# Fixing the order of the attention's matmuls on TensorE in a fused conv, attention and norm kernel

## Chip, cores, metric

The kernel runs on one core of one Trainium2 chip. The metric is the device time of one execution in microseconds (us), the median of several runs. All data are float32.

## What is computed

Eight images `x[8, 512, 32, 32]` go through two layers, each with a residual. Layer 0 normalises the image in groups, splits it by a 1x1 convolution (`cv1`) into two halves of 256 channels, runs two blocks on the second half, each a 3x3 convolution, an attention over the 1024 pixels with 4 heads of 64 channels, and a 1x1 convolution, and joins the four halves by a 1x1 convolution (`cv2`). Layer 1 normalises and applies one 1x1 convolution with a masked and permuted weight. Cut to what matters here:

```python
def bot_attention(x, qkv_w, rw, rh):
    q, k, v = (qkv[:, 0], qkv[:, 1], qkv[:, 2])
    logits = jnp.einsum('bhdi,bhdj->bhij', q, k + r) * HD ** (-0.5)
    a = jax.nn.softmax(logits, axis=-1)
    out = jnp.einsum('bhij,bhdj->bhdi', a, v)
...
    ys = [t[:, :C], t[:, C:]]
    for i in range(N):
        z = cbs(ys[-1], m_cv1_w[i], m_cv1_bn[i], 1)
        z = bot_attention(z, m_qkv_w[i], m_rw[i], m_rh[i])
        z = jax.nn.silu(bn_eval(conv2d(z, m_cv2_w[i], 0), m_cv2_bn[i]))
        ys.append(ys[-1] + z)
    return cbs(jnp.concatenate(ys, axis=1), cv2_w, cv2_bn, 0)
...
x = x + L0(groupnorm(x))
x = x + L1(groupnorm(x))
```

## The kernel before

**Units.** The attention is cut into 64 units (class `Unit`): image, block, pair of heads and half of the queries (512 of 1024). Sixteen slots of four units each follow one another; a slot is one block of one image. A unit works on eight tiles of 128 keys (`KT = 8`). Each step works on two heads at once, as two matmuls on two halves of the array: `logits` (L502) contracts 64 rows, and its two heads lie in the upper and the lower 64 rows; `values` (L548) and `finish` (L560) write 64 columns, and their two heads lie in the left and the right 64 columns. In the profile a float32 matmul shows as two instructions, so that `logits(t)` and `values(t)` are four instructions each and `finish` is four; `top` and `spread` are eight transposes each.

**What a unit does.** `logits(t)` makes two banks `lg`; ScalarE copies them to `st` (L508) and VectorE takes the running maximum `mx` (L513). `top` transposes the maximum on TensorE (`mt`, L521) and VectorE reduces it (`nm`, L522); `spread` transposes it back as a row for every key (`mb`, L529). `soften` adds it (VectorE, L533), `exponent` takes the exponential on ScalarE (L537) and adds up the sum on GpSimd (L542), `values` accumulates the output `po` over the eight tiles (L548). `finish` adds the sum over the keys on TensorE (`den`, L560), ScalarE copies it (L562), and `divide` takes the reciprocal (L566) and multiplies on VectorE.

**The emitted order.** The loop at the end of the kernel writes the work of unit `u`, of the unit `before` it and of the one after it (`nxt`) in this order: `u.top()`, filler, `u.spread()`, filler, and then, for t = 0, 2, 4, 6: at t = 0 `before.finish()`; `u.soften(t)`, `u.soften(t + 1)`; `values(t - 2)`, `values(t - 1)` (at t = 0 the last two tiles of `before`); at t = 0 `before.divide`; `nxt.logits(t)`, `nxt.logits(t + 1)`; the exponents; filler. So on TensorE, without the filler, a unit is emitted as mt, mb, den, and then four times values and logits.

**The filler.** Everything else on TensorE (the convolutions, `project`, `conv_m2`, `cv1`, `cv2` and the last layer) is cut into pieces by generators, and `advance(share)` emits as many pieces as the share of the slot's planned time asks for. The pieces between two steps of the attention are thus planned by the costs that the generators yield, and a plan's overrun can leave a place without a piece.

**Who sets the final order.** The emitted order is not the executed one. A scheduler goes through the program with its own estimate of durations, and where the next instruction in emitted order isn't ready it takes a later one of the same engine that is. Two chains of order edges (`add_manual_dep` with `IN_ORDER`, a dependency without a semaphore) already fix what may not be moved: `in_turn` for VectorE (L513, L533 and the transforms of `Spread`) and `act_turn` for ScalarE (L508, L537). TensorE has no such chain.

**Accumulators.** Of the eight banks, `ps_m` has two (`mb`), `ps_o` one (`po`) and `ps_f` five. The five of `ps_f` serve `lg` (four for a pair of tiles), `mt`, `den` and all the filler; a bank comes free when its last reader is done.

Of the kernel before, what the change touches and what calls it, by code (L numbers as in the profile page):

```python
# [20 lines left out]
IN_ORDER = mybir.DependencyInfo(mybir.DependencyClass.NoSync, mybir.DependencyReason.DATA)  # L21

P = 128
# [5 lines left out]
HALF = 512  # L29
NBLK = 2  # L30
HD = 64
NG = 16
KT = 8
# [6 lines left out]
def conv_preact_kernel(ctx: ExitStack, tc: tile.TileContext, x, cv1, cv2, mcv1, qkv, mcv2, bn, rw, rh, conv, s_in, t_in, out):  # L40
    nc = tc.nc
# [23 lines left out]
    def pair(p, tag, name):  # L65
        return p.tile([P, 2, HALF], F32, tag=tag, name=name)

    def bank(name):
        return ps_f.tile([P, HALF], F32, tag="bank", name=name)

    def half_tile(name):
        return tp.tile([P, HALF], F32, tag="t", name=name)
# [27 lines left out]
    ident = const.tile([P, P], F32, name="ident")  # L100
    make_identity(nc, ident)
    ones = const.tile([P, P], F32, name="ones")
# [79 lines left out]
    def in_turn(instruction):  # L182

        if turn:
            tc.add_manual_dep(instruction.ins, turn.pop().ins.name, IN_ORDER, reason="order of VectorE")
        turn.append(instruction)

    def act_turn(instruction):

        if act_last:  # L190
            tc.add_manual_dep(instruction.ins, act_last.pop().ins.name, IN_ORDER, reason="order of ScalarE")
        act_last.append(instruction)

    act_last = []

    class Spread:

# [288 lines left out]
    class Unit:  # L486
# [8 lines left out]
        def logits(self, t):  # L495

            if t == 0:
                self.begin()
            lg = [bank(f"lg_{self.name}_{t}_{h}") for h in range(2)]
            for h in range(2):  # L500
                r = slice(HD * h, HD * h + HD)
                nc.tensor.matmul(  # L502
                    lg[h], self.k[r, ts(t, P)], self.q[r, self.hp, ts(self.half, HALF)], start=True, stop=True
                )
            st = pair(stp, "st", f"st_{self.name}_{t}")
            self.st.append(st)
            for h in range(2):
                act_turn(nc.scalar.copy(st[:, h], lg[h]))  # L508
            if t == 1:
                self.mx = pair(one, "mx", f"mx_{self.name}")  # L510
            for h in range(2 if t else 0):
                so_far = self.st[0] if t == 1 else self.mx
                in_turn(nc.vector.tensor_tensor(self.mx[:, h], so_far[:, h], lg[h], ALU.max))  # L513

        def top(self):

            self.nm = small.tile([P, 2, 4], F32, tag="nm", name=f"nm_{self.name}")
            for h in range(2):
                mt = bank(f"mt_{self.name}_{h}").rearrange("p (c i) -> p c i", i=P)
                for c in range(4):  # L520
                    nc.tensor.transpose(mt[:, c], self.mx[:, h, ts(c, P)], ident)  # L521
                nc.vector.tensor_reduce(self.nm[:, h], mt, AX.X, ALU.max, negate=True)  # L522

        def spread(self):

            self.mb = pair(ps_m, "mb", f"mb_{self.name}")
            for h in range(2):
                for c in range(4):
                    nc.tensor.transpose(self.mb[:, h, ts(c, P)], self.nm[:, h, c : c + 1].to_broadcast([P, P]), ident)  # L529

        def soften(self, t):
            st = flat(self.st[t])
# [11 lines left out]
        def values(self, t):  # L544
            if t == 0:
                self.po = ps_o.tile([P, HALF], F32, tag="po", name=f"po_{self.name}")
            for h in range(2):
                nc.tensor.matmul(  # L548
                    self.po[HD * h : HD * h + HD],
                    self.v[:, t, ts(h, HD)],  # L550
                    self.st[t][:, h],
                    start=(t == 0),
                    stop=(t == KT - 1),
                )

        def finish(self):

            den = bank(f"den_{self.name}")
            for h in range(2):
                nc.tensor.matmul(den[HD * h : HD * h + HD], ones[:, :HD], self.acc[:, h], start=True, stop=True)  # L560
            self.rb = half_tile(f"rb_{self.name}")
            nc.scalar.copy(self.rb, den)  # L562

# [56 lines left out]
    def tables():  # L620
# [8 lines left out]
        sc = s_sb.rearrange("p a k g -> p (a k) g")  # L629
        cols = small.tile([P, 4, 2 * CT], F32, tag="cols", bufs=1, name="cols")  # L630
        top, rsum, gain, idx = (cols[:, j] for j in range(4))

        def wide(v):
            return v.unsqueeze(2).to_broadcast(full)

        e, oh, lower = scr[:, 1], scr[:, 2], scr[:, 3]
        nc.vector.tensor_reduce(top, sc, AX.X, ALU.max)
        nc.vector.tensor_tensor(e, sc, wide(top), ALU.subtract)
        nc.scalar.activation(e, e, AF.Exp)
        nc.vector.tensor_reduce(rsum, e, AX.X, ALU.add)  # L640
# [489 lines left out]
```

## Times and profile before

| what | us |
|---|---|
| three runs | 3197.96, 3199.95, 3203.04 |
| median | 3199.95 |
| the profiled execution, whole | 3202.86 |
| its span, first to last instruction | 3201.1 |
| TensorE busy | 3115.6 (97%) |
| VectorE busy | 2076.9 (65%) |
| ScalarE busy | 1718.5 (54%) |
| GpSimd busy | 1244.7 (39%) |

The granted clock of TensorE was 0.993 over the span. The groups of instructions that the change touches, of the profiled execution (two instructions a float32 matmul, and the two heads at the same time, so that the busy time is that of the pair):

| line, what | count | busy us | mean ns |
|---|---|---|---|
| L502 `lg` | 2048 | 522.4 | 617 |
| L548 `po` | 2048 | 516.6 | 607 |
| L560 `den` | 256 | 85.0 | 618 |
| L529 `mb` | 512 | 67.7 | 275 |
| L521 `mt` | 512 | 66.6 | 273 |

In a timeline of the profile a row is a run of like instructions on one engine: its start from the beginning of the span, how long it took, the engine and line, the operation, what it writes and reads, the shape, the number of instructions, and in brackets the idle time before it with what ended it. Rows of one engine may overlap a little at their ends[...]; the time that a run occupies is read from its start to the next start.

### The profile page before, as it was taken

What the parts mean: (1) busy time and instruction counts of PE and PEld (TensorE: products, weight loads), DVE (VectorE), ACT (ScalarE), POOL (GpSimd) and SP (SyncE); (2) the same over time, 40 slices, a digit from 0 to 9 for tenths busy, and PEclk for the clock granted to TensorE, in tenths of its full rate; (3) what the DMA queues carried; (4) which work ended last, traced back from release to release, by engine and by line L of the source; (5) the groups of instructions that cost most, each with busy time, mean ns of one, the idle gap of its engine ahead of it and who ended that gap; (6) DMA issues with size and microseconds to landing.
All of it is one profiled execution on the core that took longest, in us unless ns stands there. A gap on an engine that the chain in (4) does not pass through costs nothing.

```text
span 3201.1 us, 33271 instructions
## 1 busy us (share of the span) xinstructions
PE 3115.6 (97%) x11668; PEld 1527.5 (48%) x11668; DVE 2076.9 (65%) x2718; ACT 1718.5 (54%) x2347; POOL 1244.7 (39%) x971
## 2 busy tenths in 40 slices
PE   7999999999999999999999999999999999999999
PEld 3645444454445454454445454454445454453343
DVE  5446576668666676667666686667766676666642
ACT  3255765854645555544656455554645555556631
POOL 2114334445434354344434444345434443344420
PEclk9999999999999999999999999999999999999999
DMA  8851442421233232424233332424233241413366
GB/s 293 290 182 63 154 159 83 148 78 64 89 109 129 92 118 70 139 85 138 89 112 132 109 122 70 145 83 136 95 112 125 98 139 55 159 63 122 106 220 217
DMA packets 142007, 399.29 MB, mean 125 GB/s; under 512 B 13072, under 2 KB 14352, under 8 KB 141840
## 3 DMA queue, kind: packets, MB, share of 16 engines
q1 hardware_dynamic: 141120, 396.94, 36.3%
q8 instruction: 92, 1.51, 0.2%
q14 instruction: 75, 0.61, 0.1%
q10 hardware_dynamic: 720, 0.23, 0.0%
HBM read 317.42 MB, written 79.69 MB: 124 GB/s over the span
## 4 chain that ended last, share of the span: by engine, by line
PE 71%; DVE 7%; ACT 4%; DMA 2%; issue 2%; POOL 0%; SPq 0%; ACTq 0%; DVEq 0%
PE m L305 14%; PE cv L175 13%; PE po L548 11%; PE lg L502 11%; PE l L175 6%; PE qk L175 6%; PE v L397 3%; PE den L560 2%; PE m L175 2%; DVE st L533 2%; PE mb L529 2%; PE mt L521 2%; ACT st L508 1%; DVE mx L513 1%; ACT st L537 1%
## 5 line engine op out<-in xcount | busy, mean ns | idle before, releaser
L542 POOL TENSOR_TENSOR sum<-sum,st 128x512 f32<-128x512 f32 x768 | 996.8, 1323 | 705.6 <-ACT st L537 705.4
L513 DVE TENSOR_TENSOR mx<-mx,lg 128x512 f32<-128x512 f32 x768 | 477.2, 681 | 412.2 <-ACT st L508 412.2
L537 ACT ACTIVATE st<-st 128x1024 f32<-128x1024 f32 x512 | 539.1, 1068 | 341.7 <-DVE st L533 340.4
L508 ACT COPY st<-lg 128x512 f32<-128x512 f32 x1024 | 524.6, 596 | 350.5 <-PE lg L502 336.4
L533 DVE TENSOR_TENSOR st<-st,mb 128x1024 f32<-128x1024 f32 x512 | 603.2, 1212 | 66.5 <-PE mb L529 66.5
L305 PE MATMUL m<-plane,w_m 128*128 128x256 f32 x2304 | 534.4, 386 | 15.7 <-ACT cv2s L130 8.9
L548 PE MATMUL po<-st,v 128*64 128x512 f32 x2048 | 516.6, 607 | 18.3 <-ACT st L537 18.2
L502 PE MATMUL lg<-q,k 64*128 64x512 f32 x2048 | 522.4, 617 | 2.3 <-ACT y L130 1.7
L305 PEld LDWEIGHTS m<-plane,w_m 128*128 128x128 f32 x2304 | 431.3, 191 | 144.7 <-issue 47.0
L542 POOL TENSOR_TENSOR sum<-st,st 128x512 f32<-128x512 f32 x128 | 165.2, 1312 | 822.7 <-ACT st L537 822.7
L175 PE MATMUL cv<-y,w_cv 128*128 128x512 f32 x1024 | 463.2, 598 | 6.2 <-DVE mx L513 4.5
L502 PEld LDWEIGHTS lg<-q,k 64*128 64x128 f32 x2048 | 180.8, 186 | 333.5 <-issue 264.3
L175 PEld LDWEIGHTS cv<-y,w_cv 128*128 128x128 f32 x1024 | 186.3, 190 | 248.7 <-issue 230.6
L548 PEld LDWEIGHTS po<-st,v 128*64 128x64 f32 x2048 | 131.9, 137 | 328.4 <-issue 238.1
L175 PE MATMUL l<-x,w_l 128*128 128x512 f32 x512 | 235.9, 604 | 9.1 <-DVE mx L513 9.1
L175 PE MATMUL cv<-x,w_cv 128*128 128x512 f32 x512 | 235.1, 607 | 8.3 <-ACT x L165 2.4
L175 PE MATMUL qk<-z,w_qkv 128*128 128x512 f32 x512 | 234.0, 600 | 1.5 <-DVE mx L513 1.5
L566 DVE RECIPROCAL rb<-rb 128x256 f32<-128x256 f32 x128 | 215.4, 1722 | 29.5 <-ACT rb L562 29.4
L522 DVE TENSOR_REDUCE nm<-mt 128x4 f32<-128x512 f32 x128 | 82.4, 684 | 157.7 <-PE mt L521 157.7
L562 ACT COPY rb<-den 128x512 f32<-128x512 f32 x64 | 37.3, 584 | 233.4 <-PE den L560 233.4
L175 PEld LDWEIGHTS l<-x,w_l 128*128 128x128 f32 x512 | 92.8, 190 | 133.5 <-issue 110.8
L175 PEld LDWEIGHTS cv<-x,w_cv 128*128 128x128 f32 x512 | 95.0, 193 | 128.1 <-issue 107.9
(145 smaller groups left out, 2451.8 us busy)
## 6 DMA issues: line engine op xcount, KB each, us to landing
w_m<-w_m SPq DMA_DIRECT2D x96, 768.0 KB, 4.7
w_cv<-in_cv SPq DMA_DIRECT2D x90, 512.0 KB, 3.5
y<-y SPq DMA_DIRECT2D x64, 512.0 KB, 5.0
x<-in_x SPq DMA_DIRECT2D x56, 512.0 KB, 5.4
y<-y SPq DMA_DIRECT2D x64, 256.0 KB, 3.4
k<-r SPq DMA_DIRECT2D x32, 512.0 KB, 3.6
res<-y SPq DMA_DIRECT2D x32, 512.0 KB, 4.0
xr<-in_x SPq DMA_DIRECT2D x32, 512.0 KB, 4.1
```

The costliest lines, as they stand in the source:

```text
L175: nc.tensor.matmul(ps, w, moving, start=(n == 0), stop=(n == len(terms) - 1))
L305: nc.tensor.matmul(ps[:, ts(co, 256)].rearrange("p (t x) -> p t x", x=F), w[:, co, c, dx], u[:, 9 * c : 9 * c + 8, dx : dx + F], start=(j ...
L397: nc.tensor.matmul(ps[:, ts(j, P)], z[:, c, ts(4 * j4 + j, P)], w[:, c, 512 + P * hp : 512 + P * hp + P], start=(c == 0), stop=(c == IT - 1),)
L502: nc.tensor.matmul(lg[h], self.k[r, ts(t, P)], self.q[r, self.hp, ts(self.half, HALF)], start=True, stop=True)
L508: act_turn(nc.scalar.copy(st[:, h], lg[h]))
L513: in_turn(nc.vector.tensor_tensor(self.mx[:, h], so_far[:, h], lg[h], ALU.max))
L522: nc.vector.tensor_reduce(self.nm[:, h], mt, AX.X, ALU.max, negate=True)
L533: in_turn(nc.vector.tensor_tensor(st, st, flat(self.mb), ALU.add))
L537: act_turn(nc.scalar.activation(st, st, AF.Exp))
L542: nc.gpsimd.tensor_tensor(self.acc[:, h], so_far[:, h], self.st[t][:, h], ALU.add)
L548: nc.tensor.matmul(self.po[HD * h : HD * h + HD], self.v[:, t, ts(h, HD)], self.st[t][:, h], start=(t == 0), stop=(t == KT - 1),)
L566: nc.vector.reciprocal(self.rb[:, r], self.rb[:, r])
```

## The change

A third chain of order edges, `pe_turn`, is made for TensorE, and every matmul and transpose of the class `Unit` is passed through it. Each of them gets an edge to the one emitted just before it. No instruction, operand, tile or semaphore wait of the program text is added or taken away, and the filler is not in the chain. The diff, without the lines that are only indented anew:

```diff
     act_last = []
+
+    def pe_turn(instruction):
+
+        if pe_last:
+            tc.add_manual_dep(instruction.ins, pe_last.pop().ins.name, IN_ORDER, reason="order of TensorE")
+        pe_last.append(instruction)
+
+    pe_last = []
...
-                nc.tensor.matmul(
-                    lg[h], self.k[r, ts(t, P)], self.q[r, self.hp, ts(self.half, HALF)], start=True, stop=True
+                pe_turn(
+                    nc.tensor.matmul(
+                        lg[h], self.k[r, ts(t, P)], self.q[r, self.hp, ts(self.half, HALF)], start=True, stop=True
+                    )
                 )
...
-                    nc.tensor.transpose(mt[:, c], self.mx[:, h, ts(c, P)], ident)
+                    pe_turn(nc.tensor.transpose(mt[:, c], self.mx[:, h, ts(c, P)], ident))
...
-                    nc.tensor.transpose(self.mb[:, h, ts(c, P)], self.nm[:, h, c : c + 1].to_broadcast([P, P]), ident)
+                    pe_turn(
+                        nc.tensor.transpose(self.mb[:, h, ts(c, P)], self.nm[:, h, c : c + 1].to_broadcast([P, P]), ident)
+                    )
...
-                nc.tensor.matmul(
-                    self.po[HD * h : HD * h + HD],
+                pe_turn(
+                    nc.tensor.matmul(
+                        self.po[HD * h : HD * h + HD],
...
-                nc.tensor.matmul(den[HD * h : HD * h + HD], ones[:, :HD], self.acc[:, h], start=True, stop=True)
+                pe_turn(
+                    nc.tensor.matmul(den[HD * h : HD * h + HD], ones[:, :HD], self.acc[:, h], start=True, stop=True)
+                )
```

More of the change, by code (lines that the diff above doesn't have):

```diff
@@ L547, in values @@
             for h in range(2):
-                nc.tensor.matmul(
-                    self.po[HD * h : HD * h + HD],
[L550 to L553, printed above, removed]
+                pe_turn(
+                    nc.tensor.matmul(
+                        self.po[HD * h : HD * h + HD],
+                        self.v[:, t, ts(h, HD)],
+                        self.st[t][:, h],
+                        start=(t == 0),
+                        stop=(t == KT - 1),
+                    )
                 )
@@ L559, in finish @@
             for h in range(2):
-                nc.tensor.matmul(den[HD * h : HD * h + HD], ones[:, :HD], self.acc[:, h], start=True, stop=True)
+                pe_turn(
+                    nc.tensor.matmul(den[HD * h : HD * h + HD], ones[:, :HD], self.acc[:, h], start=True, stop=True)
+                )
             self.rb = half_tile(f"rb_{self.name}")
```

## The prediction

> **What bounds the kernel now.** I read the page first, then TensorE's waits, then its timeline unit by unit.
>
> ```profile
> span 3201.1 us, 33271 instructions
> ...
> PE 3115.6 (97%) x11668; PEld 1527.5 (48%) x11668; DVE 2076.9 (65%) x2718; ACT 1718.5 (54%) x2347; POOL 1244.7 (39%) x971
> ```
>
> ```profile
> PE po L548 <- ACT st L537: 18.2, 16, 2.9
> ...
> PE l L175 <- DVE mx L513: 9.1, 7, 2.1
> ```
>
> TensorE is busy for 97%, and it works through the tail too, so time that it gains in one place is not lost later as long as it is fed. Its own waits are short: the largest sum is 18.2 us, values waiting for an exponential. The other line (seven waits, 9.1 us in all, the longest 2.1) is filler of the last layer waiting for the reader of a bank that logits held; convolutions wait for it in the same way. So what counts is how well the busy time is used. A unit in emitted order (its part around mb, from TensorE's timeline at 1562 us):
>
> ```profile
> 1565.08 1.04 PE L529 MATMUL mb<-ident,nm 128*128 128x128 f32 x8
> 1565.95 1.88 PE L175 MATMUL cv<-y,w_cv 128*128 128x512 f32 x4
> 1567.76 1.08 PE L560 MATMUL den<-sum,ones 128*64 128x512 f32 x4
> 1568.67 1.89 PE L548 MATMUL po<-st,v 128*64 128x512 f32 x8
> 1570.49 1.99 PE L502 MATMUL lg<-q,k 64*128 64x512 f32 x8
> ```
>
> And one in another order (timeline from 1249 us):
>
> ```profile
> 1249.88 1.04 PE L521 MATMUL mt<-ident,mx 128*128 128x128 f32 x8
> 1250.84 1.07 PE L560 MATMUL den<-sum,ones 128*64 128x512 f32 x2
> 1251.85 1.09 PE L529 MATMUL mb<-ident,nm 128*128 128x128 f32 x8
> 1252.86 0.64 PE L560 MATMUL den<-sum,ones 128*64 128x512 f32 x1
> ...
> 1255.58 3.46 PE L502 MATMUL lg<-q,k 64*128 64x512 f32 x12
> 1259.86 2.02 PE L548 MATMUL po<-st,v 128*64 128x512 f32 x8 [0.81 <-ACT st L537]
> 1261.81 1.13 PE L502 MATMUL lg<-q,k 64*128 64x512 f32 x4
> 1262.87 5.42 PE L175 MATMUL cv<-y,w_cv 128*128 128x512 f32 x12
> ```
>
> See the counts: `den` comes as 2, 1, 1 instead of 4, and 12 and 4 `lg` stand where 8 and 8 were emitted. One head's `den` fills the wait for `nm` between mt and mb, and logits fill the wait for the exponential. In 40 of 64 units the order is the emitted one; 24 deviate.
>
> [...] a pair of heads starts 7 ns apart, and the next pair 429 ns later, the same 429 ns that one full matmul instruction takes; so a head without its partner costs its 0.86 us (two instructions) for half the work. [...] `po` to `lg` has 522 ns from start to start, 93 more than 429. [...]
>
> ```profile
> 1337.75 1.97 PE L548 MATMUL po<-st,v 128*64 128x512 f32 x2 [2.85 <-ACT st L537]
> 1339.65 6.19 PE L305 MATMUL m<-plane,w_m 128*128 128x256 f32 x18
> ```
>
> 18 instructions take 6.19 us, where 24 of them take 5.45 us elsewhere (1502.81 us); the granted clock from 1337.7 to 1344.0 is 0.51.
>
> **The change part by part.** It adds no instruction and no semaphore; it moves matmuls of `Unit` back to emitted order. They issue no DMA. Filler that takes their place is moved forward, with its readers on ScalarE and VectorE, and the weight loads behind it on SP; SP's queue isn't what TensorE waits for (all its DMA waits I found are under 0.6 us), so I cost that at nothing. What is new is that the wait of `values` or of mb now also holds the logits and `den` queued behind it, and with late logits the copies (0.6 us each) and maxima (0.68 us) of the next unit. It costs time only where no filler is at hand.
>
> (a) The split `den`. From den to lg 4.74 us (1250.84 to 1255.58), mb included; in order 0.87 (mb) + 2.73 (1567.76 to 1570.49) = 3.60. With 0.09 more at mt (0.96 against 0.87), 1.23 us a unit. Fourteen units have it, at 543, 722, 884, 1250, 1440, 1480, 1610, 1975, 2163, 2203, 2334, 2700, 2888 and 2926 us; 756 has a variant.
>
> (b) Logits ahead of values. Whole tiles (12 and 4): 3.47 + 1.06 us against 2 x 1.91, 0.71 more, in three units (1250, 1975, 2700), which also wait 0.81, 0.81 and 0.99 us there. One lone head (10 and 6, five units at 934, 1480, 1660, 2203, 2384): 1.05 + 1.91 against 1.91, 1.05 more.
>
> (c) One head of the last `values` before mt (1338, 2064, 2788): the fence above.
>
> What comes in the place? The reduction that mb waits for ended at 1251.81 and mb began at 1251.85: without `den`, TensorE has 1.0 us to fill there, and 2.35 us (4.27 from the start of lg to po, less 1.92) after the first logits. If filler has an open bank and pieces left, it fills both. I read this from the filler row after each place. In the units at 1250, 1975 and 2700 a group of 16 has done 4 and has 12 left: I take all, 1.23 + 0.71 + 0.87 = 2.8, x3 = 8.4. At 1480 and 2203 a product of the 3x3 convolution is open: 1.23 + 1.05 = 2.3, x2 = 4.6. At 884, 1610 and 2334 (12 left of 16): 1.23 x3 = 3.7. At 934, 1660 and 2384, product open: 1.05 x3 = 3.2. At 543, 1440, 2163 and 2888 only 4 of a group of 8 are left: they move between mt and mb and are then missing after the logits. If the next group gets a bank, the gain is 1.23 + 0.37 (the wait there now) = 1.6; if not, mb comes 0.7 us later (two matmuls of 0.86 in the place of 1.0) and all behind it, -0.7. I take 0.5, x4 = 2.0.
>
> (c) bounds: if the 3x3 matmuls could start at once, 1339.65 - 1334.89 = 4.8 us, plus 1.9 for nine pairs at 0.21 us of slow clock, less 0.5 for the head done later: 6.2. But all five banks are taken by logits until about 1338 to 1339 (copies from 1337.61), so I take 1.5, x3 = 4.5, and keep 0 and 6.2.
>
> The units at 722, 756 and 2926 have the largest excess (7.8, 2.2 and 3.6 us over the 17.75 us that an ordered unit's attention takes on TensorE, and 4.7 us of waits), but VectorE sets them: it is busy 23.78 us of the 24.00 from 731 to 755. I take 2 for all three; bounds -4 and 12.
>
> Sum: 8.4 + 4.6 + 3.7 + 3.2 + 2.0 + 4.5 + 2.0 = 28.4 us, against the profiled execution's 3202.9, so 3174.5; that execution was 2.9 us over the median of the runs, so in terms of the median about 3172. Since the scheduler places all later filler anew, the bank waits elsewhere (about 23 us on `mx`) will shift; +-10 us without a sign.
>
> **The rivals.** *All of it is won:* every unit comes to 17.75 us. Excess over all deviating units 36.5, waits for exponentials in them 9, (c) another 9: about 50 us less, 3150. For it: TensorE is the bound nearly everywhere. Against: the three units where VectorE is.
>
> *Starved behind the fixed order (slower):* the logits hold four of five filler banks, so that once the open group is finished TensorE stands for the whole 2.35 us between logits and values, where it had logits or `den` to do. Price a unit: 2.35 idle, plus half of 1.9 (a slow clock follows some waits of this length, not all), less the 1.23 saved: +2.1. In the 14 units of (a), +29: 3229. It decides once more than about a third of the units starve (1.23 against 2.1). For it: filler waits on `mx` exist already, up to 2.1 us. Against: of the 15 units listed above where filler must fill, an open group follows in 11.
>
> *Little changes:* the scheduler's places were idle time of TensorE anyway, filler moves up and is missing later: 3194 to 3206, middle 3200. For it: 40 units are in order already.
>
> **How the numbers follow.** My forecast, 3155 to 3193 around 3172: 0.58. All won: 0.12. Little: 0.15. Starved: 0.15. A measurement of this kernel can tell about 0.2% from no change, 6.4 us. Faster 0.58 + 0.12 and a share of the edge of "little" = 0.71; same 0.14; slower 0.15. The range goes from 3150 (0.05 below) to 3204, up to where "little" ends, with 0.15 left out above.
>
> **What would show it.** In the changed kernel's timeline every unit should read mt, mb, den x4, po x8, lg x8 without a lone head, and TensorE's 17.75 us a unit should hold everywhere that the clock is full; filler should stand between mt and mb in the units of (a). The wait of `po` for `st` should fall from 18.2 us to under 12. The forecast is wrong if waits of TensorE at po, mb or filler on `mx` grow by more than the 36 us that the order saves, or if TensorE's slow stretches multiply.

## The result, and the profile after

| | before | after |
|---|---|---|
| median of 18 runs each, us | 3200.12 | 3190.07 |
| lowest and highest, us | 3195.81, 3205.56 | 3186.11, 3196.62 |
| the profiled execution, us | 3202.86 | 3187.86 |
| its span, us | 3201.1 | 3186.1 |

The ratio is 0.9968, with a 95% interval of 0.9962 to 0.9975: the change makes the kernel 10 us faster, where 28 were forecast; 3190 lies at the upper end of the forecast's 3155 to 3193. A second set of runs on another chip (the run "changed" below) gave 3193.01 against 3203.65, 0.9963 (0.9951 to 0.9976).

The page of the changed kernel, span and busy time:

```profile
span 3186.1 us, 33275 instructions
...
PE 3083.2 (97%) x11668; PEld 1522.2 (48%) x11668; DVE 2077.2 (65%) x2718; ACT 1717.3 (54%) x2347; POOL 1243.3 (39%) x971
```

TensorE is busy for 32.4 us less than before (3115.6), on the same 11668 instructions, and the profiled span shrank by 15.0 us. So the order saves TensorE nearly the 36 us that the prediction names, and about half of that comes back as idle time (32.4 less 15.0 is 17.4 us). TensorE's waits in the changed kernel (what waited for what: sum, times, longest, in us):

```profile
PE po L561 <- ACT st L549: 14.8, 11, 3.7
...
PE l L175 <- DVE mx L523: 9.7, 7, 2.0
PE m L313 <- DVE x2r L487: 9.0, 3, 3.6
...
PE cv L175 <- DVE mx L523: 8.8, 7, 1.8
PE po L561 <- DVE mx L523: 7.7, 9, 2.3
```

The wait of values for the exponential fell only from 18.2 to 14.8 us. Two rows are new: values put down to `mx` (7.7 us), and the 3x3 convolutions waiting for `x2r`, the reader of a bank (9.0 us). The wait of the 1x1 convolutions `cv` on `mx` rose from 6.6 to 8.8. Summed from one unit's mt to the next over 63 units, TensorE's waits are 59.1 us before and 75.2 after, the attention's own instructions 1160.5 and 1127.1, the filler 1610.5 and 1611.2.

The unit that the prediction showed out of order (at 1250 us), in the changed kernel's TensorE timeline:

```profile
1248.59 1.04 PE L531 MATMUL mt<-ident,mx 128*128 128x128 f32 x8
1249.46 1.02 PE L175 MATMUL cv<-y,w_cv 128*128 128x512 f32 x2
1250.32 1.04 PE L540 MATMUL mb<-ident,nm 128*128 128x128 f32 x8
1251.29 1.08 PE L575 MATMUL den<-sum,ones 128*64 128x512 f32 x4
1252.20 1.89 PE L561 MATMUL po<-st,v 128*64 128x512 f32 x8
1254.02 1.99 PE L511 MATMUL lg<-q,k 64*128 64x512 f32 x8
1255.93 1.99 PE L175 MATMUL cv<-y,w_cv 128*128 128x512 f32 x4
1258.29 2.02 PE L561 MATMUL po<-st,v 128*64 128x512 f32 x8 [0.37 <-DVE mx L523]
```

This is the order as emitted: mt, mb, `den` x4, then eights of values and logits, with two instructions of filler between mt and mb where one head of `den` stood. Now read two distances. From mt to the first logits it is 5.43 us; before, it was 5.71 (1249.88 to 1255.58, rounded). From the first logits to the values after them it is 4.27 us (1254.02 to 1258.29); before, it was 4.28 (1255.58 to 1259.86), although four more logits stood there then. The first distance shrank by a quarter of what the split `den` cost, and the second didn't shrink at all. The experiments ask who holds it.

Two theories. **A:** in the units that the change puts in order (the moved units), the chain behind mb (VectorE adds, ScalarE copies and takes exponentials, VectorE takes the maxima) sets the pace, and time that TensorE saves turns into waiting. **B:** TensorE sets the pace there as elsewhere, and the gain is lost in the filler's new places. Units are counted from 0: unit 23 is the one above, 15, 31 and 47 are those at 884, 1610 and 2334 us of the kernel before, 27 is that at 1440, 30 is in order in both kernels (1562 us). The length of a unit is the time from its mt to the mt of the next.

### The profile page after: what moved, and what is told of

It reads as the page before. It is cut to its first block, busy times and chain, and to the rows that moved or that the text cites. A ratio compares the mean times of both kernels' runs of the same rounds, so it can differ in the third digit from the quotient of the medians.

```text
span 3186.1 us, 33275 instructions
## 1 busy us (share of the span) xinstructions
PE 3083.2 (97%) x11668; PEld 1522.2 (48%) x11668; DVE 2077.2 (65%) x2718; ACT 1717.3 (54%) x2347; POOL 1243.3 (39%) x971
## 4 chain that ended last, share of the span: by engine, by line
PE 70%; DVE 8%; ACT 4%; issue 3%; DMA 2%; POOL 0%; SPq 0%; ACTq 0%; DVEq 0%
PE m L313 13%; PE cv L175 13%; PE po L561 11%; PE lg L511 11%; PE l L175 6%; PE qk L175 6%; PE v L405 3%; PE m L175 2%; DVE st L545 2%; PE mb L540 2%; PE mt L531 2%; PE den L575 2%; ACT st L518 1%; DVE mx L523 1%; ACT st L549 1%
## 5 line engine op out<-in xcount | busy, mean ns | idle before, releaser
L554 POOL TENSOR_TENSOR sum<-sum,st 128x512 f32<-128x512 f32 x768 | 996.1, 1322 | 701.3 <-ACT st L549 701.1
L549 ACT ACTIVATE st<-st 128x1024 f32<-128x1024 f32 x512 | 539.1, 1068 | 342.9 <-DVE st L545 341.5
L561 PE MATMUL po<-st,v 128*64 128x512 f32 x2048 | 497.6, 606 | 22.6 <-ACT st L549 14.8
L511 PE MATMUL lg<-q,k 64*128 64x512 f32 x2048 | 511.3, 617 | 1.6 <-ACT y L130 1.6
```

What stands on the lines that cost most here:

```text
L511: nc.tensor.matmul(lg[h], self.k[r, ts(t, P)], self.q[r, self.hp, ts(self.half, HALF)], start=True, stop=True)
L549: act_turn(nc.scalar.activation(st, st, AF.Exp))
L554: nc.gpsimd.tensor_tensor(self.acc[:, h], so_far[:, h], self.st[t][:, h], ALU.add)
L561: nc.tensor.matmul(self.po[HD * h : HD * h + HD], self.v[:, t, ts(h, HD)], self.st[t][:, h], start=(t == 0), stop=(t == KT - 1),)
```

## The experiments

### One part of the chain at a time

part_top, the chain of order edges without logits and values, and part_steps, without mt, mb and `den`:

```diff
part_top
-                pe_turn(nc.tensor.matmul(lg[h], ...))
+                nc.tensor.matmul(lg[h], ...)
-                pe_turn(nc.tensor.matmul(self.po[...], ...))
+                nc.tensor.matmul(self.po[...], ...)
part_steps
-                    pe_turn(nc.tensor.transpose(mt[:, c], ...))
+                    nc.tensor.transpose(mt[:, c], ...)
-                    pe_turn(nc.tensor.transpose(self.mb[:, h, ts(c, P)], ...))
+                    nc.tensor.transpose(self.mb[:, h, ts(c, P)], ...)
-                pe_turn(nc.tensor.matmul(den[...], ...))
+                nc.tensor.matmul(den[...], ...)
```

> Only mt, mb and den are in the chain; logits and values are left free. Theory A (after mb the unit's time is set by VectorE and ScalarE, so that TensorE time saved behind mb becomes a wait): the split den is mended, 1.23 us of TensorE time in each of 14 units, but only about 0.3 us a unit is kept, 4 us in all: about 3196, ratio to before 0.9985. Theory B (TensorE time counts wherever it is saved, and the order of den saves most of it): 14 x 1.23 = 17 us, cut by the same third as the whole change kept, so about 6 to 11 us: 3189 to 3194.

> Only logits and values are in the chain; mt, mb and den are left free. Theory A: the early values before mt (about 4.8 us in three units of the profile after) and part of the logits ahead are kept: 5 to 8 us, about 3193. Theory B: 7.4 us of TensorE time for the logits, and the values, cut as the whole was: 2 to 5 us, about 3196.

part_top took 3205.59 us against 3204.40: 1.0003 (0.9994 to 1.0012), no gain, and neither theory had said so. Its timeline at unit 31:

```profile
1610.84 1.04 PE L529 MATMUL mt<-ident,mx 128*128 128x128 f32 x8
1611.81 1.07 PE L558 MATMUL po<-st,v 128*64 128x512 f32 x2
1612.81 1.09 PE L538 MATMUL mb<-ident,nm 128*128 128x128 f32 x8
```

With `den` held back, a lone head of values goes into the gap between mt and mb, at the same cost. In all fourteen units with a split, mt to the first logits stays at 5.71 us. part_steps took 3202.26: 0.9988 (0.9979 to 0.9998), by the ratio 3.9 us less than before, by the medians 2.1; `den` stays split there, and of the units with a split only 23, 28, 39, 44 and 55, which have logits ahead of values too, get shorter (unit 23: 43.38 us before, 42.52, and 41.93 with the whole chain; unit 15: 50.04, 50.03, 49.76). The halves bring at most 3 us together and the whole 10: a half chain leaves another step free to take the same gap.

### More work for TensorE, in moved and in unmoved units

`den` is issued twice, in 15 units that the change reordered (pad_moved) or in 15 that it left as they were (pad_ordered). One doubling was reckoned at 0.91 us of TensorE; in the traces it adds 0.86 (unit 30: 48.86 us for 48.00), 12.9 in all.

```diff
-        def finish(self):
+        def finish(self, twice=False):
...
-            for h in range(2):
+            for h in range(4 if twice else 2):
...
-                    before.finish()
+                    before.finish(4 * s + j in TWICE)
```

> The changed kernel, with den issued twice (same result, 0.91 us more of TensorE time) in the 15 units that were out of order before and have filler: 13.7 us of added TensorE time. Theory A: these units have idle TensorE time between mb and their next wait, so little of it counts: 2 to 5 us over the changed kernel, 3192 to 3195. Theory B: TensorE is the bound here too, 11 to 14 us: 3201 to 3204.

> The same doubled den in 15 units that were in emitted order before and have no wait of TensorE in the profile: 13.7 us of added TensorE time. Both theories: it counts nearly in full, 11 to 14 us over the changed kernel, 3201 to 3204. If it counts for little here too, TensorE is not the bound that the busy share suggests, and both fall.

pad_ordered: 3208.14 against 3204.40, 1.0015 (1.0008 to 1.0022), so about 15 us over the changed kernel (0.9968). TensorE sets the pace in the units that were in order: fourteen of the 15 are 0.86 us longer or more. pad_moved: 3206.38, 1.0008 (0.9999 to 1.0017), about 13 us over the changed kernel. That is B's number and A missed. Unit by unit it is less simple: the doubled `den` lies ahead of the first logits, which come 0.86 us later (in unit 27 6.29 us after mt, not 5.43), and the 4.27 us from there to the values stay. So it delays the chain itself, and twelve units are 0.7 to 0.9 us longer. In units 15, 31 and 47 it costs 0.2 us each: a filler wait falls from 1.8 to 1.1 us and swallows the rest. The experiment put its load where both theories pay for it, so it doesn't decide between them.

### Does the bank come free too late?

The running maximum reads the copy `st` and no longer `lg`, so that a bank of logits is free after ScalarE's copy. max_copy is the changed kernel with this, max_copy_free the kernel before.

```diff
-                in_turn(nc.vector.tensor_tensor(self.mx[:, h], so_far[:, h], lg[h], ALU.max))
+                in_turn(nc.vector.tensor_tensor(self.mx[:, h], so_far[:, h], st[:, h], ALU.max))
```

> The changed kernel with the running maximum read from ScalarE's copy st instead of from the logits' bank lg, so that a bank comes free with the copy and does not wait for VectorE. Theory A in its form 'the bank is held by the late maximum': TensorE's waits of filler for mx (about 22 us in the profile after) go, 10 to 20 us faster than the changed kernel, 3170 to 3180. Theory A in its form 'VectorE and ScalarE pace the steps anyway': the waits turn into waits of values for the exponential, within 5 us of 3190. Theory B (the scheduler's new placing is what cost): no clear change.

> The kernel before with the same maximum from the copy and no order of TensorE. If banks held by the maximum are what let the order's saving go to waste, the difference between max_copy and this one is well above the 10 us that the order gives by itself, 20 to 30 us. If not, it is about 10 again.

Both are far slower: 3388.59 against 3207.29, 1.0568 (1.0551 to 1.0585), and 3367.85, 1.0504 (1.0486 to 1.0523). The groups tell why; first the changed kernel's, then max_copy's (busy us, mean ns of one):

```profile
L523 DVE TENSOR_TENSOR mx<-mx,lg 128x512 f32<-128x512 f32 x768 | 477.6, 681 | 406.2 <-ACT st L518 406.2
```

```profile
L523 DVE TENSOR_TENSOR mx<-mx,st 128x512 f32<-128x512 f32 x768 | 936.6, 1276 | 310.9 <-ACT st L518 310.8
```

The same maximum costs 1276 ns in place of 681, which is 459 us of VectorE, and says nothing on the banks. Neither theory had priced that, and the question is left open in this form. With so slow a maximum the order of TensorE even costs time: max_copy is 20.7 us longer than max_copy_free, where a gain of 10 to 30 was expected. No run shows why.

### den first

`before.finish()` is emitted between `u.top()` and `u.spread()`, inside the chain, so that a whole pair of `den` fills the wait for `nm`.

```diff
             u.top()
             clock.tick(0.9)
+            if before:
+                before.finish()
+                clock.tick(0.9)
...
-                if before and t == 0:
-                    before.finish()
-                    clock.tick(0.9)
```

> The changed kernel with finish emitted between top and spread, so that both heads of den fill the wait for the reduction before mb. Theory A: mb starts no later, and 0.9 us less lies between mb and the logits, which the chain over ScalarE and VectorE sees in the 15 units or so without spare filler: 5 to 12 us faster than the changed kernel, 3178 to 3185. Theory B: TensorE does the same work, filler only changes places: within 3 us of 3190.

It took 3228.14 against 3207.29: 1.0068 (1.0054 to 1.0081), 21 us slower than before and some 32 slower than the changed kernel, against both theories. Unit 30, in den_first's timeline:

```profile
1573.25 1.04 PE L531 MATMUL mt<-ident,mx 128*128 128x128 f32 x8
1574.21 1.08 PE L575 MATMUL den<-sum,ones 128*64 128x512 f32 x4
1575.22 1.98 PE L175 MATMUL cv<-y,w_cv 128*128 128x512 f32 x4
1577.04 1.04 PE L540 MATMUL mb<-ident,nm 128*128 128x128 f32 x8
```

From the start of `den` to the start of the filler it is 1.01 us; where `den` is followed by values, which use the same halves of the array, it is 0.91 (1251.29 to 1252.20 above). `den` alone among whole-array work thus took about 0.1 us more on each side, ahead of it 0.96 us from mt, where filler follows mt after 0.87, and `po`, with filler ahead of it, took 1.87 us to the logits (1579.73 to 1581.60) in place of 1.82 (1252.20 to 1254.02 above). Attention on TensorE takes 18.0 to 18.1 us in place of 17.7 to 17.8 in the units in order, and unit 30 is 48.35 us, not 48.00. Twenty-five units in order are longer by 0.3 to 0.4, 9 us in all; units 3, 9, 19, 35 and 51 add 16 (1.7 to 6.3 us each), for a reason that wasn't looked for. In units 7, 15, 23, 27 and their like, den_first is 0.1 to 0.4 us shorter than the changed kernel, which is theory A's sign at a small size.

### Is it VectorE?

The reciprocals of `divide` are left out, so that the output is multiplied by the sum.

```diff
-            nc.vector.reciprocal(self.rb[:, r], self.rb[:, r])
```

> The changed kernel without the two reciprocals of divide (the output is multiplied by the sum instead of divided by it): 3.4 us less of VectorE in each of 64 units, nothing less on TensorE. Theory A: in the 20 units or so that VectorE paces up to 3.4 us is won, on the whole 20 to 40 us: 3150 to 3170. Theory B: VectorE is busy for 65% and not the bound, 0 to 8 us: 3182 to 3190.

3190.50 against 3207.29, 0.9943 (0.9923 to 0.9963): by the ratios 6 to 8 us better than the changed kernel (0.9963 and 0.9968), though the intervals touch, for 198 us less of VectorE (2077.2 to 1879.6). VectorE is thus not the pace in general. Units 15, 31 and 47 gain 0.8 us each, unit 27 gains 1.2; units 23, 28 and 16 nothing.

### The changed kernel again, and a filler held back

"changed" is the changed kernel itself, for a base on the chip of hold and the first pair after it. In hold, in 12 of the moved units, the next filler is put behind the first logits by one more order edge, so that nothing stands between mt and mb; the filler's matmuls pass through `held_back`.

```diff
                     nxt.logits(t + 1)
+                    if t == 0 and 4 * s + j in HOLD:
+                        hold.append(pe_last[-1])
...
+    def held_back(instruction):
+        if hold:
+            tc.add_manual_dep(instruction.ins, hold.pop().ins.name, IN_ORDER, reason="filler behind the logits")
```

> The changed kernel once more, on the chip of the three that follow: ratio to before about 0.997, as on record.

> The changed kernel with one more order edge in 12 of the units that were out of order: the next filler stays behind the first logits instead of moving up between mt and mb. Theory A2 (a unit's time goes by when its first logits come and by the fixed 4.3 us from there to the values, so that filler which moved up between mt and mb costs 0.86 us there and is missing behind the logits): TensorE idles about 1.1 us before mb, but logits come 0.2 us earlier and the filler fills the wait of the values, 0.2 to 1.1 us a unit: 4 to 9 us faster than the changed kernel. Theory B2 (TensorE time is what counts, an idle microsecond before mb is lost): 8 to 12 us slower than the changed kernel.

hold took 3190.15 against 3203.65, 0.9962 (0.9948 to 0.9976), the changed kernel's own ratio. Both theories missed. TensorE's timeline of unit 27, first in the kernel before, then in the changed kernel, then in hold:

```profile
1445.53 1.99 PE L502 MATMUL lg<-q,k 64*128 64x512 f32 x8
1447.45 1.98 PE L175 MATMUL l<-x,w_l 128*128 128x512 f32 x4
1449.80 2.02 PE L548 MATMUL po<-st,v 128*64 128x512 f32 x8 [0.37 <-ACT st L537]
```

```profile
1435.47 1.02 PE L175 MATMUL l<-x,w_l 128*128 128x512 f32 x2
...
1440.02 1.99 PE L511 MATMUL lg<-q,k 64*128 64x512 f32 x8
1441.94 1.12 PE L175 MATMUL l<-x,w_l 128*128 128x512 f32 x2
1444.29 2.02 PE L561 MATMUL po<-st,v 128*64 128x512 f32 x8 [1.23 <-ACT st L549]
```

```profile
1435.83 1.25 PE L551 MATMUL mb<-ident,nm 128*128 128x128 f32 x8 [0.35 <-DVE nm L543]
...
1439.74 1.99 PE L522 MATMUL lg<-q,k 64*128 64x512 f32 x8
1441.65 1.98 PE L175 MATMUL l<-x,w_l 128*128 128x512 f32 x4
1444.01 2.02 PE L572 MATMUL po<-st,v 128*64 128x512 f32 x8 [0.37 <-DVE mx L534]
```

In hold the two filler instructions stand behind the logits, and the values wait 0.37 us, not 1.23: the 0.86 us is exactly those two. Logits to values is 4.27 us in all three, whatever filler stands between them. It is so in units 7, 11, 23, 27, 39, 43 and 59 of these kernels. That put the question to ScalarE. A second limit lies close behind: in den_first unit 27's logits come earlier still (4.86 us after mt), and the values don't follow (4.85 us after the logits):

```profile
1456.42 1.99 PE L511 MATMUL lg<-q,k 64*128 64x512 f32 x8
...
1461.27 1.94 PE L561 MATMUL po<-st,v 128*64 128x512 f32 x8 [0.94 <-DVE q L584]
```

There they wait for `q`, the product in `divide`, which must have read the one bank of `po` before the next values write it.

### Exponentials ahead of the copies

ScalarE around those logits, in the changed kernel (unit 27):

```profile
1441.24 2.05 ACT L518 COPY st<-lg 128x512 f32<-128x512 f32 x4 [2.20 <-PE lg L511]
1443.15 2.04 ACT L549 ACTIVATE st<-st 128x1024 f32<-128x1024 f32 x2
```

ScalarE is idle for 2.20 us, then copies four banks of logits, and only then takes the exponential that the values wait for (the first ends at about 1444.2, the values start at 1444.29). `act_turn` keeps copies and exponentials as emitted, and `nxt.logits` is emitted ahead of `u.exponent`. exp_early emits the exponents of tiles 0 and 1 ahead of `nxt.logits(0)` in all units, exp_early_free does the same on the kernel before.

```diff
-                if t:
-                    u.exponent(t)
+                u.exponent(t)
+                if not t:
+                    u.exponent(t + 1)
...
-                if not t:
-                    u.exponent(t)
-                u.exponent(t + 1)
+                if t:
+                    u.exponent(t + 1)
```

> The changed kernel with the first two exponentials of a unit emitted, and so run on ScalarE, ahead of the copies of the first logits, where ScalarE is idle for about 2 us. Theory A2: the values behind the first logits no longer wait for them (about 0.4 us in 8 units, 1.2 in 4, more in 2): 6 to 14 us faster than the changed kernel. Theory C (VectorE's work from mb on paces these units): the wait comes back at the next bank, within 4 us of the changed kernel.

> The kernel before, without the order of TensorE, with the same early exponentials. Theory A2: logits no longer find a gap to move into ahead of the values; the split den stays: faster than before by 5 to 12 us, and the order brings another 3 to 8 on top. Theory C: as before within 4 us.

exp_early took 3201.36 against 3203.65, 0.9994 (0.9986 to 1.0002); exp_early_free 3216.21, 1.0035 (1.0023 to 1.0046). Both are worse than their bases as a whole, by 8 to 13 us, which neither theory had said, but the moved units do what theory A2 said: logits to values falls from 4.27 to 3.83 us in units 7, 23, 27 and their like, and units 15, 31 and 47 go from 49.7 to 47.7 us each. What loses lies elsewhere, 24 us of it in units 0, 2, 3 and 4. ScalarE's table loads, in the changed kernel and then in exp_early:

```profile
L549 ACT ACT_TABLE_LOAD x110 | 141.1, 1283 | 2.0
```

```profile
L549 ACT ACT_TABLE_LOAD x130 | 166.8, 1283 | 2.4
```

With the 20 on L130 that go with them it is 40 more loads, 51 us of ScalarE. The activations of the convolutions (silu) stand between an early exponential and the next ones, and in the changed kernel's trace a load of 1.28 us stands at each of the 205 changes from an exponential (L549) to an activation of L130 or back. Units 0, 3 and 4 have 2, 4 and 4 more loads and are 5, 8 and 8 us longer than in the changed kernel's trace; 17, 33 and 49 have 2 more and are 1.7 longer. At 1.28 us each the loads are 2.6 to 5.1 us in units 0, 3 and 4, so that they are not all of it.

So the last pair does it only in units 7, 11, 15, 16, 23, 27, 31, 32, 39, 43, 47, 48, 55, 59 and 60, chosen from exp_early's trace: exp_some on the changed kernel, exp_some_free on the kernel before.

```diff
-                if t:
+                early = t == 0 and 4 * s + j in EARLY
+                if t or early:
                     u.exponent(t)
+                if early:
+                    u.exponent(t + 1)
...
-                if not t:
+                if not t and not early:
...
-                u.exponent(t + 1)
+                if not early:
+                    u.exponent(t + 1)
```

> The changed kernel with the two first exponentials early only in 15 of the units that were out of order before, all others as in the changed kernel. If the fixed stretch from logits to values swallowed what the order saved in these units, shortening it there gives it back: in the profile of exp_early these units came to 12 to 14 us less than in the changed kernel, so 8 to 14 us faster than the changed kernel, ratio to before 0.992 to 0.994. If the early exponentials only shift the wait, within 3 us of the changed kernel.

> The kernel before, without the order of TensorE, with the same early exponentials in the same 15 units. If the stretch from logits to values is what sets these units, it gains by itself, 4 to 10 us on before, and the order's part on top (exp_some against this) stays near 10 us or grows. If TensorE's order is what sets them, this is no faster than before.

exp_some: 3177.30 (3168.65 to 3181.20) against 3199.89, 0.9923 (0.9910 to 0.9935). It beats both kernels, the changed one by 13 or 14 us (0.9923 against 0.9963 and 0.9968, on other chips). exp_some_free: 3191.68, 0.9973 (0.9962 to 0.9984). On top of early exponentials the same order of TensorE brings 14.4 us (3191.68 to 3177.30), alone 10; the intervals don't separate the two, but the units do. In 15, 31 and 47 the order alone won 0.3 us, and here it wins 1.14. The starts of units 31 and 32 in exp_some_free (48.86 us apart), then in exp_some (47.72):

```profile
1605.19 1.04 PE L521 MATMUL mt<-ident,mx 128*128 128x128 f32 x8
...
1654.05 1.04 PE L521 MATMUL mt<-ident,mx 128*128 128x128 f32 x8
```

```profile
1603.08 1.04 PE L531 MATMUL mt<-ident,mx 128*128 128x128 f32 x8
...
1650.80 1.04 PE L531 MATMUL mt<-ident,mx 128*128 128x128 f32 x8
```

Unit 27 in exp_some, ScalarE and TensorE:

```profile
1439.05 2.01 ACT L549 ACTIVATE st<-st 128x1024 f32<-128x1024 f32 x2
1441.35 2.05 ACT L518 COPY st<-lg 128x512 f32<-128x512 f32 x4 [0.30 <-PE lg L511]
```

```profile
1440.14 1.99 PE L511 MATMUL lg<-q,k 64*128 64x512 f32 x8
1442.06 1.13 PE L175 MATMUL l<-x,w_l 128*128 128x512 f32 x2
1443.97 1.94 PE L561 MATMUL po<-st,v 128*64 128x512 f32 x8 [0.79 <-DVE q L584]
```

The exponentials now use ScalarE's idle time, the values come 3.83 us after the logits, and they wait for `q`, as in den_first. In this unit and in 7, 43 and 59 the order therefore still wins only 0.3 us (39.39 to 39.10 in unit 27), and most of what it saves comes back as the 0.79 us before the values. An earlier `divide` was not tried. exp_some has only six more table loads than the changed kernel.

## Why the prediction was wrong in size

The direction, TensorE's saving and the units in which it falls were right; what that saving is worth was not. The sum was 28.4 us where the units gave 11. By the prediction's own terms, from the unit lengths (mt to next mt) of the two profiled executions:

| units at | forecast | attention on TensorE saved | waits added | unit time won |
|---|---|---|---|---|
| 1250, 1975, 2700 | 8.4 | 5.3 | -0.1 | 4.5 |
| 1480, 2203 | 4.6 | 4.1 | 0.8 | 3.0 |
| 884, 1610, 2334 | 3.7 | 3.4 | 2.5 | 0.9 |
| 934, 1660, 2384 | 3.2 | 2.9 | 1.4 | 1.3 |
| 543, 1440, 2163, 2888 | 2.0 | 4.4 | 3.3 | 1.3 |
| 722, 756, 2926 | 2.0 | 8.4 | 8.7 | 0.1 |
| sum | 23.9 | 28.5 | 16.6 | 11.1 |
| early values, (c) | 4.5 | 4.4 | 2.7 | 4.8, and -1.8 in the second profile |

Where the time won is not the saving less the added waits, the filler took a little more or less time. All other units together changed by 0.7 us. The second profile of the changed kernel repeats the sum (12.2). In the fifteen units of the first five rows the forecast was 21.9, TensorE saved 20.1, 8.0 of it came back as waits, and 11.0 were won.

**The failed step** is "If filler has an open bank and pieces left, it fills both ... I take all": the sum counts TensorE's saved time as time won, and puts the waits that come back at nothing; they came to 8.0 of 20.1 us in those fifteen units. The filler does stand between mt and mb in the twelve units of (a) that the prediction didn't give to VectorE, two instructions or four short ones (at 543 and its like four long ones were foreseen, and two of them stay behind the logits). But that is not extra room. In most of these units the order saves 1.14 us from mt to the first logits, of which 0.86 is filled with filler and 0.28 is won (5.71 to 5.43). Those 0.86 us of filler are then missing later, and whether that matters is decided by who ends the unit, which the prediction didn't ask, except in the three units where it saw VectorE busy throughout. In unit 27 it is missing at once, and the wait of the values grows by the same 0.86 (0.37 to 1.23). In units 15, 31 and 47, with plenty of filler, the values do come 1.14 us earlier, and most of it is lost some 17 us further on. Before, and then after, at 1610 us:

```profile
1612.46 1.09 PE L529 MATMUL mb<-ident,nm 128*128 128x128 f32 x8
...
1639.27 1.12 PE L175 MATMUL cv<-y,w_cv 128*128 128x512 f32 x2 [0.91 <-DVE mx L513]
```

```profile
1605.19 1.04 PE L540 MATMUL mb<-ident,nm 128*128 128x128 f32 x8
...
1631.95 1.56 PE L175 MATMUL cv<-y,w_cv 128*128 128x512 f32 x3 [1.75 <-DVE mx L523]
```

From mb to the bank that the last maxima release it is 26.81 and 26.76 us: this stretch keeps its length, and TensorE's 0.86 us became 0.84 us more of waiting. The prediction named that wait ("the bank waits elsewhere ... will shift") and gave it no sign. The early exponentials show that ScalarE's order holds it: with them the wait is gone, and the order wins its full 1.14 us in these three units (48.86 in exp_some_free to 47.72); without them 0.3. VectorE's work is part of the same stretch: without the reciprocals the three units were 0.8 us shorter. At 543 and its like the saving still comes back as a wait, now for `q`.

**Point by point.** (a) 1.23 us a unit: TensorE saved 1.14 where (a) stands alone (0.96 at 543). The 0.09 is missing because `mb` to `den` takes 0.97 us in order (1250.32 to 1251.29), where the sum has 0.87: the delay next to `den` moves with it from mt to mb. (b) In the three units with whole tiles ahead, 1.5 us each and not 2.8: TensorE saved 1.8 of the 1.94 that (a) and (b) promise, but waits of 0.8 remain: logits to values stayed at 4.27, with 0.37 of waiting in it, and 0.48 came up later, at a convolution. These 0.87 us a unit were counted as won. The lone heads: at 934, 1660 and 2384 TensorE saved 0.98 of 1.05 each, and 0.4 of it was won. The units at 543 and its like: 0.5 forecast, 0.3 won, for the reason given there. (c) No gain is shown. The wait fell away at the values and came back at the convolutions behind them, 3.56 us for `x2r`, the reader of a filler's bank; the prediction had feared banks held by logits. What it costs varies from one execution to the next; the same place in the changed kernel and in its second profile:

```profile
1336.46 4.15 PE L313 MATMUL m<-plane,w_m 128*128 128x256 f32 x18 [3.56 <-DVE x2r L487]
```

```profile
1334.50 5.81 PE L313 MATMUL m<-plane,w_m 128*128 128x256 f32 x18 [3.56 <-DVE x2r L487]
```

Same program, same wait, and the 18 instructions behind it take 4.15 us at a granted clock of 1.00 or 5.81 us at 0.71. The three such places account for 6.6 of the 8.6 us between these two profiled spans, and such differences can make up the distance between 15 us (the profiled pair) and 10 us (the medians).

**The signs it named.** Every unit reads mt, mb, `den` x4, po x8, lg x8: yes. 17.75 us of attention a unit: yes, 17.7 to 18.1 in 57 of 63 units. `po` waiting for `st` under 12 us: no, 14.8, and 7.7 more under another releaser's name. "The forecast is wrong if waits ... grow by more than the 36 us": they grew by 16, and half of the saving was gone, since each microsecond of it counts against the gain.

**The rivals.** "Starved behind the fixed order" had the right mechanism at a smaller size: a wait after the logits, at most 0.9 us more a unit in the fifteen units of the first five rows, where it gave 2.35, and the granted clock of unit 27 stays at 1.00. Of the units of (a) and (b), only the one at 2926 us, which the prediction had given to VectorE, waits longer than it saves: it is 1.9 us longer in the first profile and 0.8 in the second. "Little changes" had the reason, filler that moves up and is missing later, for the seven units at 543 and 884 and their like, which won 0.3 us each (0.4 at 543).

**What stays open.** Whether an earlier free bank alone would win the wait in units 15, 31 and 47 (max_copy changed VectorE's cost and couldn't tell); whether an earlier `divide` would win the rest in unit 27 and its like; and why the order costs time when the maximum is slow.

## What to carry to other kernels

A stretch in which an engine is busy for 97% can still be paced by another: before a saving on it is summed, find in each stage the pair of events whose distance stays the same (logits to values in unit 27 here, 4.27 us in the kernels before, changed, hold and pad_moved), and count the saving only up to the next such pair. Filler that moves up into a gap is no gain by itself; it is a loan, paid back where the filler is next wanted. Where two engines' orders are fixed, look at the second one's order first: moving exponentials ahead of copies in 15 units brought 8 us where the whole order of TensorE brought 10, and the two together 23. That is more than their sum in units 15, 31 and 47, where each alone leaves the other's limit standing; over the whole kernel the surplus is within the noise. The 15 units were picked from a trace; in all units the same move lost time.

## What the hardware showed

- VectorE's 128x512 maximum of two float32 inputs took 681 ns on the mean with one input in a bank and 1276 (median 1453, 666 at best) with both in SBUF, the on-chip memory; GpSimd's sums, which run beside it, went from 1322 to 1502 ns in the same run (max_copy). In the trace the time goes with GpSimd's work: of the 768 maxima with two SBUF inputs the 268 that no GpSimd instruction overlaps took 683 ns on the mean, and the 341 with GpSimd at work for nine tenths of their time or more took 1623. With one input in a bank (the changed kernel) it made no difference, 681 and 682.
- A table load on ScalarE takes 1283 ns, on the mean in each group of the changed kernel (222 loads in all). Where its neighbours were ready it stood close between them: in exp_early an exponential ends at 397.15, the load runs from 397.16 to 398.44, and the silu starts at 398.46.
- A lone `den` between whole-array matmuls costs about 0.1 us at each side (0.96 us from mt to `den` against 0.87 from mt to filler, and 1.01 against 0.91 from `den` to the next start), and 0.35 us a unit as a whole (den_first, unit 30).
- After equal waits of 3.56 us the next 18 matmuls took 4.15 us at a granted clock of 1.00 or 5.81 us at 0.71, in two executions of one program. In the kernel before, the granted clock behind a wait of 2.85 us was 0.51 in one place (1337.7 to 1344.0) and 1.00 in another (1150.47 to 1154.0), and behind 2.10 us it was 0.57 (2053.28 to 2057.20), behind 2.13 us 1.00 (613.59 to 617.0).
